# Graph attention and hypergraph convolution on pairs of graphs: row scales through DRAM, score rows and squares transposed, attention moved inside a product chain

## The chip, the cores and the metric

The kernel runs on one core of one Trainium2 chip. The metric is the device time of one execution, in microseconds (us), on the slowest (here the only) core. A single-core program has no second die to compare with, so runs are compared by their spread.

## The reference, cut to what matters

128 graphs of 128 nodes with 512 features. A layer of graph attention (8 heads of 64), then a layer of hypergraph convolution (hidden size 1024), each with a residual and a layer norm. Shortened:

```
feats   = x W                                   # per head: 64 features
e       = leaky_relu(e_self[i] + e_neigh[j])    # scores, 8 heads of 128x128
att     = softmax(e - 1e10*(1 - adj))
y       = layernorm(x + relu(att feats + b))
# hypergraph convolution; w = first row of adj, H = (adj != 0)
Dn      = 1 / sum_e H[n,e] w[e]                 # one scale per node (row)
Be      = 1 / sum_n H[n,e]                      # one scale per edge
S       = diag(Dn) H diag(Be) H^T               # 128x128, used twice
h       = layernorm(relu(S (y W1) + b1))
out     = layernorm(y + S (h W2) + b2 + y)
```

## The kernel before: the parts that the change and the argument touch

The kernel works on pairs of graphs. Every step of a pair is entered with a lag (in periods) and a time in the period, and the program is laid out in the order of these numbers, 39.2 us to a period; so four or five pairs are in work at once, and each engine executes its own instructions strictly in that order. The large products (pf, ph, py) are Strassen-like chains of seven products; ScalarE copies three partial results per chain out of PSUM.

```
# S: rows scaled in SBUF by VectorE, transposed by PE, R = S^T copied out by ScalarE
hD[:, g] = (a[:, g] != 0) * dn[:, g]            # nodes, VectorE, 2 per pair
pa[g]    = PE transpose(hD[:, g])               # 2 per pair
hDT      = ScalarE copy(pa)
pd[g]    = matmul(hB[:, g], hDT[:, g])          # hB = edge-scaled H^T
R        = ScalarE copy(pd)
# score rows: PE transposes e_neigh (16 rows of 128), VectorE copies them out of PSUM,
# two writes to DRAM, then each row is read back by all 128 partitions
rows = copy(pr[:16])
for g in range(2):
    dma rd[g] <- rows[8g:8g+8]                  # 8 partitions x 4 runs of 128 B
for g in range(2):
    dma nb[:, g] <- rd[g] broadcast             # 4 KB runs
# then: GpSimd adds the mask to nb, ScalarE applies leaky relu, VectorE takes the largest
# squares: pm[:, g] = matmul(sq[:, g, 0], mean1)        # one column, 1/DH
# py chain: seven products py(1..7); ScalarE copies out py after the 1st, 3rd and 5th that PE does
# next pair's blocks: four loads xb (x) and four loads ab (adjacency)
```

The steps from load to score rows are all DMAs that one engine, SP, issues in program order.

## Time and profile before

| | before |
|---|---|
| time, median of 3 runs | 2601.62 us (2600.46 to 2602.16) |
| busy: PE, VectorE, ScalarE, GpSimd | 97, 78, 60, 66% |
| steady period (one pair) | 39.12 us, PE busy in all of it |
| chain that ended last | PE 96% |

These are the SP lines of one period of the kernel before (start, length, line, output and input, number of DMAs; the length is that of issuing, with waits inside a group included):

```profile
1087.64 2.47 SPq L110 DMA_DIRECT2D xb<-in_x_dram  x4
1090.16 2.13 SPq L115 DMA_DIRECT2D ab<-in_adj_dram  x4
1093.92 0.62 SPq L470 DMA_DIRECT2D rd<-rows  x2
1095.16 0.82 SPq L479 DMA_DIRECT2D nb<-rd  x2
```

The reader is to see that the score rows are issued 1.6 us after the four ab loads are done, and that the first read of them back follows 1.24 us after the first write began. In the median of 60 periods it is 1.24 us as well, and the four ab loads take 1.94 us.

### The profile page before, as it was taken

Reading aid. Unit: us, or ns where it says so; the run is one execution under the profiler, and the core shown is the slowest. Engines: PE = TensorE matmul, PEld = TensorE weight load, DVE = VectorE, ACT = ScalarE, POOL = GpSimd, SP = SyncE. Lnnn points to the kernel's source line nnn. Section 1 sums busy time; section 2 is a strip of 40 time slices with the busy share of each in tenths; the row PEclk is TensorE's granted clock in tenths of the full one; section 3 lists DMA queues with packets and bytes.
Section 4 is the critical chain, followed back from the end, with each engine's and each line's share of the span. In section 5 each row is a group of like instructions: output and inputs, shape, how many; then the busy total and the mean of one; then the engine's idle time right before and its main releaser. Section 6 shows DMA issues by size and latency. Waiting matters only on the chain.

```text
span 2601.9 us, 48690 instructions
## 1 busy us (share of the span) xinstructions
PE 2530.2 (97%) x16624; PEld 2298.1 (88%) x16624; DVE 2027.5 (78%) x4584; ACT 1555.9 (60%) x4425; POOL 1720.3 (66%) x1809
## 2 busy tenths in 40 slices
PE   4799999999999999999999999999999999999997
PEld 2699999999999999999899999999999999999986
DVE  5788788787788787787787788787787787787773
ACT  2566566566566566566566566566565575575562
POOL 3566766766766766766767767667767667767653
PEclk9899999999999999999999999999999999999998
DMA  6344444443444444443443444444544534534430
GB/s 162 110 130 132 135 130 132 135 130 123 144 130 127 140 129 126 142 130 121 147 129 121 148 127 122 148 126 122 150 124 123 151 122 125 151 120 127 147 106 17
DMA packets 332668, 335.64 MB, mean 129 GB/s; under 512 B 99442, under 2 KB 265346, under 8 KB 332420
## 3 DMA queue, kind: packets, MB, share of 16 engines
q1 hardware_dynamic: 328724, 331.46, 42.3%
q8 instruction: 132, 2.16, 0.3%
q10 hardware_dynamic: 3696, 1.06, 0.2%
q14 instruction: 116, 0.95, 0.1%
HBM read 232.27 MB, written 100.14 MB: 128 GB/s over the span
## 4 chain that ended last, share of the span: by engine, by line
PE 96%; DVE 1%; DMA 1%; issue 1%; POOL 0%; ACT 0%; SPq 0%; POOLq 0%; DVEq 0%; ACTq 0%
PE pyX L419 17%; PE phX L698 17%; PE pfX L419 9%; PE phW L698 9%; PE pyW L419 8%; PE pav L572 8%; PE pz L663 4%; PE phY L698 4%; PE pfW L419 4%; PE pyY L419 4%; PE pq L819 4%; PE pfY L419 2%; PE pd L379 1%; PE pm L792 1%; PE pa L329 1%
## 5 line engine op out<-in xcount | busy, mean ns | idle before, releaser
L290 ACT COPY py<-pyX 128x257 f32<-128x257 f32 (+1 forms) x192 | 71.7, 374 | 561.1 <-PE pyX L419 557.7
L698 PEld LDWEIGHTS phX<-zS,w_sb 128*128 128x128 f32 x3072 | 363.1, 192 | 31.2 <-issue 31.2
L698 PE MATMUL phX<-zS,w_sb 128*128 128x128 f32 x3072 | 374.2, 275 | 0.7 <-issue 0.7
L492 POOL TENSOR_TENSOR nb<-nb,neg 128x512 f32<-128x512 f32 x256 | 320.1, 1271 | 75.7 <-DMA nb<-rd 75.7
L499 ACT ACTIVATE nb<-nb,ft 128x128 f32<-128x128 f32 x1024 | 326.4, 392 | 53.1 <-POOL nb L492 53.0
L749 POOL TENSOR_TENSOR sq<-sq 128x512 f32<-128x512 f32 (+2 forms) x384 | 321.6, 837 | 36.3 <-ACT sq L738 21.1
L513 ACT ACTIVATE nb<-nb,nm 128x128 f32<-128x128 f32 x1024 | 320.4, 395 | 0.0
L619 POOL TENSOR_TENSOR rso<-veo,mhalf 128x2 f32<-128x2 f32 x64 | 44.8, 700 | 375.9 <-DVE veo L617 375.9
L572 PEld LDWEIGHTS pav<-ft,eT 128*128 128x128 f32 x2048 | 253.3, 193 | 11.8 <-DVE eT L534 3.4
L419 PE MATMUL pyX<-w_sb,h 128*128 128x257 f32 (+1 forms) x1024 | 253.6, 390 | 0.2
L572 PE MATMUL pav<-ft,eT 128*128 128x65 f32 x2048 | 247.6, 271 | 3.4 <-DVE eT L534 3.2
L419 PE MATMUL pyX<-w_sb,hS 128*128 128x257 f32 (+1 forms) x1024 | 244.6, 381 | 3.2 <-POOL hS L401 3.2
L419 PE MATMUL pyW<-w_sb,hS 128*128 128x256 f32 x1024 | 242.3, 378 | 0.0
L728 ACT ACTIVATE h<-h,b_sb 128x128 f32<-128x128 f32 x768 | 239.4, 392 | 1.4 <-DVE h L713 1.4
L686 POOL TENSOR_TENSOR zS<-zT 128x256 f32<-128x256 f32 x128 | 93.5, 730 | 210.3 <-ACT zT L675 210.3
L419 PEld LDWEIGHTS pyX<-w_sb,hS 128*128 128x128 f32 x1024 | 194.6, 190 | 32.2 <-POOL hS L401 3.6
L419 PEld LDWEIGHTS pyW<-w_sb,hS 128*128 128x128 f32 x1024 | 193.9, 189 | 28.0
L596 POOL TENSOR_TENSOR y<-y,b_bc 128x512 f32<-128x512 f32 x128 | 186.3, 1456 | 28.5 <-DVE rden L586 24.6
L419 PEld LDWEIGHTS pyX<-w_sb,h 128*128 128x128 f32 x1024 | 185.7, 191 | 21.7 <-ACT py L290 0.4
L505 DVE TENSOR_REDUCE nm<-nb 128x4 f32<-128x512 f32 x256 | 174.2, 681 | 23.3 <-ACT nb L499 22.9
L290 ACT COPY ph<-phX 128x512 f32<-128x512 f32 x192 | 112.4, 585 | 88.9 <-PE phX L698 88.9
L534 DVE STREAM_TRANSPOSE eT<-eb 128x512 f32<-128x512 f32 x252 | 163.0, 683 | 0.1
(125 smaller groups left out, 5846.8 us busy)
## 6 DMA issues: line engine op xcount, KB each, us to landing
nb<-rd SPq DMA_DIRECT2D x128, 512.0 KB
ed<-nb SPq DMA_DIRECT2D x126, 512.0 KB
eb<-ed SPq DMA_DIRECT2D x504, 128.0 KB
xb<-in_x_dram SPq DMA_DIRECT2D x256, 128.0 KB
x<-in_x_dram SPq DMA_DIRECT2D x64, 512.0 KB
out_dram<-o SPq DMA_DIRECT2D x64, 512.0 KB
a<-in_adj_dram SPq DMA_DIRECT2D x64, 128.0 KB
w<-in_adj_dram SPq DMA_DIRECT2D x128, 64.0 KB
```

The source lines that it names most:

```text
L290: nc.scalar.copy(t[:, :n], s[kind, "X"][:, :n])
L419: nc.tensor.matmul(to[:, :n], lhs[:, k, :], rhs[:, k, :n], start=bool(start) and k == 0, stop=(k == nk - 1), skip_group_check=True,)
L492: nc.gpsimd.tensor_tensor(t, t, neg[:, :, None, :].to_broadcast([P, NB, HH, B]), op=ALU.add)
L499: nc.scalar.activation(t, t, AF.Prelu, bias=s["ft"][:, g, h, 0:1], alpha=SLOPE)
L505: nc.vector.tensor_reduce(s["nm"][:, g, hs], scores(p, s, g, hs).rearrange("p b h j -> p h b j"), AX.XY, ALU.max, negate=True,)
L513: nc.scalar.activation(t, t, AF.Exp, bias=s["nm"][:, g, h:h + 1])
L534: nc.vector.transpose(s["eT"][:, g, hs, :].rearrange("p h (b i) -> p h b i", b=NB), s["eb", g][:, :, hs, :].rearrange("p b h j -> p h b j"),)
L572: nc.tensor.matmul(t[:, h * (U + 1):(h + 1) * (U + 1)], s["eT"][:, g, q * HH + h, :], s["ft"][:, g, q * HH + h, 2:], start=True, stop=True,)
L596: nc.gpsimd.tensor_tensor(s["y"][:, g, :], s["y"][:, g, :], b0_bc, op=ALU.add)
L698: nc.tensor.matmul(to[:, m * N:(m + 1) * N], w[:, k, m * P:(m + 1) * P], rhs[:, k, :], start=bool(start) and m == 0 and k == 0, stop=(k == ...
L728: nc.scalar.activation(dst[:, k, :], src[:, k, :], AF.Relu, bias=b1_sb[:, c:c + 1])
L749: nc.gpsimd.tensor_tensor(t[:, :n, :], t[:, :n, :], t[:, n:2 * n, :], op=ALU.add)
```

## The change

Its intent is to take small work off PE, which is the bound. Four parts: (1) S comes from H^T alone, and the row scale Dn is multiplied in along the columns when R leaves PSUM; for that the 256 scales of a pair go through DRAM and are read back by all partitions. (2) Score rows are turned by VectorE's 32x32 block transpose instead of PE. (3) The squares are transposed by PE and summed by VectorE. (4) The two late attention blocks (pav) and the py chain are interleaved otherwise. The diff, cut to its core:

```diff
-        s["hD"] = ...                       # and its two VectorE scalings     (1)
+        s["dn"] = dn
+    @step(0, 16.0)
+    def write_nodes(p, s):
+        s["dd"] = dram.tile([2, N], F32, ...)
+        nc.sync.dma_start(s["dd"].rearrange("g n -> n g"), s["dn"])
+    @step(1, 20.0)
+    def spread_nodes(p, s):
+        s["dnb"] = work.tile([P, 2 * N], F32, ...)
+        nc.sync.dma_start(s["dnb"], s["dd"].rearrange("g n -> (g n)").partition_broadcast(P))
-    def transpose_nodes ...                 # pa, 2 PE transposes
-    def d_evict ...                         # ScalarE copy
-                s["hB"][:, g, :], s["hDT"][:, g, :],
+                s["hB"][:, g, :], s["hT"][:, g, :],
-        nc.scalar.copy(R, pd)
+        nc.vector.tensor_tensor(R, pd, s["dnb"], op=ALU.mult)
 ...
-        pr = PE transpose; rows = copy(pr)  # two writes of 8 partitions       (2)
+        rows = work.tile([P, B], F32, ...)
+        nc.vector.transpose(rows, e_self and e_neigh columns of ft)
+        for b in range(NB):                 # four writes of 16 partitions
+            nc.sync.dma_start(s["rd"][b], rows[b * B + 2 * H:(b + 1) * B])
 ...
-            nc.tensor.matmul(s["pm"][:, g:g + 1], s["sq"][:, g, 0, :], mean1)  # (3)
+            nc.tensor.transpose(s["pm"][:, g * N:(g + 1) * N], s["sq"][:, g, 0, :], ident)
+        nc.vector.tensor_reduce(ve, s["pm"], AX.X, ALU.add)
 ...
-    (..., ((1, 0), 24.2), ((1, 1), 25.0)):  attend                           # (4)
+    (..., ((1, 0), 25.95), ((1, 1), 26.8)): attend
-    chain("py", 3, (26.0, 27.8, 29.5, 31.2, 33.0, 35.5, 37.2, 27.9, 31.4, 34.75), ...
+    chain("py", 3, (24.2, 29.4, 27.7, 32.9, 31.2, 35.35, 37.1, 26.2, 29.6, 33.1), ...
-    T = 39.2
+    T = 38.6
```

More of the change, by code (lines that the diff above doesn't have):

```diff
@@ L176 @@
     nc.gpsimd.memset(mhalf, -0.5)
-    mean1 = const.tile([P, 1], F32, name="mean1")
-    nc.gpsimd.memset(mean1, 1.0 / DH)
     fts = []
@@ L313, in nodes @@
         nc.vector.scalar_tensor_tensor(dn, dd, 0.0, dn, op0=ALU.is_gt, op1=ALU.mult)
-        s["hD"] = work.tile([P, 2, N], F32, tag="hD", name=f"hD_{p}")
-        for g in range(2):
-            nc.vector.tensor_scalar(
-                s["hD"][:, g, :], a[:, g, :], 0.0, dn[:, g:g + 1], op0=ALU.not_equal, op1=ALU.mult
-            )
+        s["dn"] = dn
+    @step(0, 16.0)
+    def write_nodes(p, s):
+        s["dd"] = dram.tile([2, N], F32, tag="dd", name=f"dd_d_{p}")
+        nc.sync.dma_start(s["dd"].rearrange("g n -> n g"), s["dn"])
+    @step(1, 20.0)
+    def spread_nodes(p, s):
+        s["dnb"] = work.tile([P, 2 * N], F32, tag="dnb", name=f"dnb_{p}")
+        nc.sync.dma_start(
+            s["dnb"], s["dd"].rearrange("g n -> (g n)").partition_broadcast(P)
+        )
     @step(0, 38.4)
@@ L323, in mask @@
         nc.gpsimd.tensor_scalar(s["neg"], s["a"], -1.0, BIG, op0=ALU.add, op1=ALU.mult)
-    @step(1, 1.78)
-    def transpose_nodes(p, s):
-        s["pa"] = bank(f"pa_{p}")
-        for g in range(2):
-            nc.tensor.transpose(s["pa"][:, g * N:(g + 1) * N], s["hD"][:, g, :], ident)
     @step(1, 31.0)
@@ L345 @@
     at(1, 5.3, x_transpose, 1)
-    @step(1, 2.6)
-    def d_evict(p, s):
-        s["hDT"] = work.tile([P, 2, N], F32, tag="hDT", name=f"hDT_{p}")
-        nc.scalar.copy(s["hDT"].rearrange("p g n -> p (g n)"), s["pa"][:, :2 * N])
     @step(1, 3.4)
@@ L373, in scale_edges @@
             )
-    @step(1, 34.6)
+    @step(1, 34.7)
     def propagator(p, s):
@@ L379, in propagator @@
             nc.tensor.matmul(
-                s["pd"][:, g * N:(g + 1) * N], s["hB"][:, g, :], s["hDT"][:, g, :],
+                s["pd"][:, g * N:(g + 1) * N], s["hB"][:, g, :], s["hT"][:, g, :],
                 start=True, stop=True,
             )
-    @step(1, 35.3)
+    @step(1, 35.8)
     def r_evict(p, s):
         s["R"] = work.tile([P, 2, N], F32, tag="R", name=f"R_{p}", bufs=3)
-        nc.scalar.copy(s["R"].rearrange("p g n -> p (g n)"), s["pd"][:, :2 * N])
+        nc.vector.tensor_tensor(
+            s["R"].rearrange("p g n -> p (g n)"), s["pd"][:, :2 * N], s["dnb"], op=ALU.mult
+        )
     def first_sums(s, key, name, a, i, engine, tag):
@@ L447, with blocked, spread_rows @@
     at(1, 23.4, f_sum, 1, 0, None, "X")
-    @step(1, 24.95)
-    def transpose_scores(p, s):
-        s["pr"] = bank(f"pr_{p}")
-        nc.tensor.transpose(
-            s["pr"][:2 * H, :N], s["ft"][:, :, :, 1].rearrange("p g h -> p (g h)"), ident
-        )
-    def blocked(p, t):
-        dims = "(h b j) -> {}b h j" if p == 0 else "(b h j) -> {}b h j"
-        if len(t.shape) == 2:
-            dims = "p " + dims.format("p ")
-        return t.rearrange(dims.format(""), b=NB, h=H)
-    @step(1, 25.4)
-    def spread_rows(p, s):
-        rows = work.tile([2 * H, N], F32, tag="rows", name=f"rows_{p}")
-        nc.vector.tensor_copy(rows, s["pr"][:2 * H, :N])
-        rd = s["rd"] = dram.tile([2, NB, H, B], F32, tag="rd", name=f"rd_{p}")
-        for g in range(2):
+    def blocked(p, t):
+        dims = "p (h b j) -> p b h j" if p == 0 else "p (b h j) -> p b h j"
+        return t.rearrange(dims, b=NB, h=H)
+    @step(1, 25.0)
+    def spread_rows(p, s):
+        rows = work.tile([P, B], F32, tag="rows", name=f"rows_{p}")
+        nc.vector.transpose(
+            rows.rearrange("p (c x) -> p c x", c=2),
+            s["ft"][:, :, :, :2].rearrange("p g h c -> p c (g h)"),
+        )
+        shape = [2 * H, NB, B] if p == 0 else [NB, 2 * H, B]
+        s["rd"] = dram.tile(shape, F32, tag="rd", name=f"rd_{p}")
+        for b in range(NB):
             nc.sync.dma_start(
-                blocked(p, rd[g].rearrange("b h j -> (b h j)")).rearrange("b h j -> h b j"),
-                rows[g * H:(g + 1) * H].rearrange("h (b j) -> h b j", b=NB),
+                s["rd"][:, b, :] if p == 0 else s["rd"][b],
+                rows[b * B + 2 * H:(b + 1) * B],
             )
@@ L478, in neighbours @@
         for g in range(2):
-            nc.sync.dma_start(
-                s["nb"][:, g, :],
-                s["rd"][g].rearrange("b h j -> (b h j)").partition_broadcast(P),
-            )
+            hs = slice(g * H, (g + 1) * H)
+            dst, src = s["nb"][:, g, :], s["rd"]
+            if p == 0:
+                src = src[hs].rearrange("h b j -> (h b j)")
+            else:
+                dst = dst.rearrange("p (b x) -> p b x", b=NB)
+                src = src[:, hs, :].rearrange("b h j -> b (h j)")
+            nc.sync.dma_start(dst, src.partition_broadcast(P))
     def scores(p, s, g, hs):
@@ L553 @@
     for (g, q), tm, (lag, tl), (lagx, tx), te, tt in (
-        ((0, 0), 31.0, (1, 32.5), (1, 34.8), 2.7, 18.1), ((0, 1), 33.0, (1, 35.4), (1, 37.3), 4.6, 18.15),
-        ((1, 0), 34.2, (1, 38.0), (2, 2.0), 7.8, 21.5), ((1, 1), 35.4, (2, 6.0), (2, 7.3), 7.9, 21.55),
+        ((0, 0), 31.0, (1, 32.4), (1, 33.9), 2.7, 18.1), ((0, 1), 32.2, (1, 34.0), (1, 36.7), 4.6, 18.15),
+        ((1, 0), 34.2, (1, 37.5), (2, 2.0), 7.8, 21.5), ((1, 1), 35.4, (2, 6.0), (2, 7.3), 7.9, 21.55),
     ):
@@ L575, in attend @@
             )
-    for (g, q), t in (((0, 0), 20.65), ((0, 1), 20.7), ((1, 0), 24.2), ((1, 1), 25.0)):
+    for (g, q), t in (((0, 0), 20.65), ((0, 1), 20.7), ((1, 0), 25.95), ((1, 1), 26.8)):
         at(2, t, attend, g, q)
@@ L592 @@
     at(2, 22.5, attended, 0)
-    at(2, 26.4, attended, 1)
+    at(2, 27.9, attended, 1)
     def add_bias(p, s, g):
@@ L598 @@
     at(2, 24.1, add_bias, 0)
-    at(2, 28.0, add_bias, 1)
+    at(2, 29.2, add_bias, 1)
     def residual(p, s, g):
@@ L625, in normalize @@
         )
-    at(2, 27.6, residual, 0)
-    at(2, 30.0, residual, 1)
-    at(2, 31.7, rstds, "a")
-    @step(2, 32.6)
+    at(2, 26.2, residual, 0)
+    at(2, 30.7, residual, 1)
+    at(2, 32.7, rstds, "a")
+    @step(2, 34.95)
     def first_shift(p, s):
@@ L642, in first_output @@
         )
-    at(2, 37.0, first_output, 0)
-    at(2, 37.1, first_output, 1)
+    at(2, 35.7, first_output, 0)
+    at(2, 35.75, first_output, 1)
     def skip(p, s, g):
@@ L752 @@
         for level in range(3):
-            at(3, ((17.0, 17.1, 17.2), (26.0, 28.5, 28.6))[g][level], squares, g, level)
+            at(3, ((17.0, 17.1, 17.2), (26.0, 27.3, 28.0))[g][level], squares, g, level)
     def h_sums(p, s, i):
@@ L767, in weigh @@
         rows_product(s, i, halves(s["h"], KH // 2), s["hS"], w2_sb, QU, KH // 2, 1, to, start)
-    chain("py", 3, (26.0, 27.8, 29.5, 31.2, 33.0, 35.5, 37.2, 27.9, 31.4, 34.75), weigh,
+    chain("py", 3, (24.2, 29.4, 27.7, 32.9, 31.2, 35.35, 37.1, 26.2, 29.6, 33.1), weigh,
           QU, 1)
@@ L781, in y_sum @@
             nc.vector.tensor_tensor(dst, s["py", i][:, :n], s["py", where][:, :n], op=ALU.add)
-    at(3, 29.6, y_sum, 0, 0, 0, "Y")
-    at(3, 35.4, y_sum, 1, 1, 2, "W")
+    at(3, 31.3, y_sum, 0, 0, 0, "Y")
+    at(3, 34.9, y_sum, 1, 1, 2, "W")
     at(4, 0.1, y_sum, 0, 1, 1, "W")
-    at(3, 37.3, y_sum, 1, 0, None, "X")
-    @step(3, 35.0)
+    at(3, 37.2, y_sum, 1, 0, None, "X")
+    @step(3, 34.8)
     def sum_squares(p, s):
@@ L791, in sum_squares @@
         for g in range(2):
-            nc.tensor.matmul(
-                s["pm"][:, g:g + 1], s["sq"][:, g, 0, :], mean1, start=True, stop=True
-            )
+            nc.tensor.transpose(s["pm"][:, g * N:(g + 1) * N], s["sq"][:, g, 0, :], ident)
     @step(3, 36.0)
@@ L801, in h_rstd @@
         ve = small.tile([P, 2], F32, tag="ve", name=f"veh_{p}")
-        nc.vector.tensor_tensor(ve, s["pm"][:, :2], m2, op=ALU.subtract)
+        nc.vector.tensor_reduce(
+            ve, s["pm"][:, :2 * N].rearrange("p (g f) -> p g f", g=2), AX.X, ALU.add
+        )
+        nc.vector.scalar_tensor_tensor(
+            ve, ve, 1.0 / DH, m2, op0=ALU.mult, op1=ALU.subtract
+        )
         nc.vector.tensor_scalar(ve, ve, 0.0, EPS, op0=ALU.max, op1=ALU.add)
@@ L860, in shift @@
             if lag == 0:
-                return 2.5 if time < 20.0 else 0.0
+                return 2.5 if time < 12.0 else 0.0
             if lag == 1 and 4.0 < time < 10.0:
@@ L866, in shift @@
         if p == 1 and lag == 1:
-            if time < 3.0:
-                return -3.0
+            if time < 4.0:
+                return -6.0
             return -17.5 if time < 10.0 else -13.0 if time < 12.0 else -23.1 if time < 26.0 else 0.0
```

## The prediction

> **What bounds the kernel now.** One core, so no dies to compare; the granted clock is 0.992. I read the busy shares first, then PE's waits over the whole run, then the busy times of one steady period, then the chain of waits inside it.
>
> ```profile
> PE 2530.2 (97%) x16624; PEld 2298.1 (88%) x16624; DVE 2027.5 (78%) x4584; ACT 1555.9 (60%) x4425; POOL 1720.3 (66%) x1809
> ...
> 1025.69:1064.81 39.12, 39.12 (x260) 35.70 (x261) 31.02 (x72) 24.20 (x71) 26.84 (x29) 1.00 0.42 132
> ```
>
> The second line is one period (one pair of graphs; there are 64): PE is busy 39.12 of 39.12 us, VectorE 31.02, ScalarE 24.20, GpSimd 26.84, the DMA engines 42%. PE's waits are all start and end effects, each counted once or twice:
>
> ```profile
> PE pa L329 <- DVE hD L316: 29.9, 1, 29.9
> PE pz L663 <- ACT y L640: 17.5, 1, 17.5
> PE pyX L419 <- POOL hS L401: 3.2, 1, 3.2
> PE pav L572 <- DVE eT L534: 3.2, 1, 3.2
> ```
>
> So from about 92 us to 2523 us the time is the sum of PE's slots, and nothing else counts unless it makes PE wait. The chain of waits gives those slots (start, length); these are the ones the change touches, with their neighbours:
>
> ```profile
> 1029.26 1.78 PE pz L663 x16
> 1031.04 0.22 PE pa L329 x2
> 1031.26 1.79 PE phX L698 x16
> ...
> 1049.94 1.73 PE pav L572 x16
> ...
> 1053.50 0.84 PE pav L572 x8
> 1054.34 0.11 PE pr L452
> 1054.45 0.84 PE pav L572 x8
> 1055.29 1.79 PE pyX L419 x8
> ...
> 1062.29 1.73 PE pyX L419 x8
> 1064.03 0.44 PE pd L379 x4
> 1064.47 0.34 PE pm L792 x4
> 1064.81 1.84 PE pyX L419 x8
> ```
>
> Three things to see. A matmul is two instructions (pd: 2 products, x4), a transpose one (pa: 2, x2), and both cost 0.11 us an instruction at 128 columns (0.44/4, 0.22/2). A product of 128x256 takes 1.73 for 8, or 0.217 each. And a product is longer by what a short predecessor could not hide: pyX is 1.73 after a long one, 1.79 after pav (65 columns), 1.84 after pm (1 column).
>
> **What the Trainium skill says.** "TensorE: Matmul & The Clock Gate", section "LDWEIGHTS (loading the stationary operand)", gives a load as its columns over 1.2, that is 107 ns for 128 columns, and its step-by-step section lets the next load run under the current matmul. The trace agrees: pav streams only 65 columns and yet takes 1.73/16 = 0.108 us, a load's time, and pm with its single column has 0.34 + (1.84 - 1.73) = 0.45 for four loads. The same page, "Part 4: PE-mode transpose", warns that the clock gate does not open for transposes alone; here pa's slots are as short as pd's, so between matmuls that does not show. "VectorE: DVE Perf Modes", section "Why PSUM operands drop a tier", leaves fp32 from PSUM at one element a cycle; VectorE's sums from PSUM took 0.42 us at 256 columns and 0.685 at 512, a slope of 0.97 elements/ns, which fits, and I use these rows for the new PSUM reads. "SBUF — State Buffer", section "SBUF: two separate sides", says that VectorE with two SBUF inputs and a GpSimd operation lock each other out of a port pair. The trace has the like: first_shift on 128x2 elements lasts 1.20 us on average beside GpSimd's score additions, but 0.16 at 2548.94 when GpSimd is idle.
>
> **The change part by part.** All in us per period.
> 1. S from H^T alone. Two PE transposes (pa) go: -0.22. The propagator still has 2 products of 128x128, 0.44. The row scale is now multiplied in as PSUM is left, so ScalarE loses two copies (0.38 + 0.37), VectorE loses the hD scaling (two, 0.48 together) and gets a 128x256 product from PSUM (0.42). The scales go through DRAM: one write of 256 single floats and one broadcast read of 128 KB. They are written about a period before use, so I charge them nothing.
> 2. Score rows by VectorE's transpose. PE's pr goes: -0.11. But pr with its 128 columns also hid one load between two pav blocks: 0.84 + 0.11 + 0.84 = 1.79, whereas 16 in one block cost 1.73. Net -0.06. VectorE loses a copy (0.28) and gets a 128x32 transpose: from 0.434 at 256 elements and 0.683 at 512, about 0.434 - 224 x 0.00097 = 0.22.
> 3. Squares. pm with its after-effect, 0.45, becomes two transposes of 128 columns, 0.22, after which the next load is hidden: -0.23. VectorE pays a 128x256 reduction from PSUM, about 0.43 (from 0.68 at 512), and a tiny operation takes the place of a tiny one.
> 4. Attention inside the py chain. The four pav blocks and the py products stay the same, and each of the two pav stretches is still followed by one uncovered load. The move gives cover: the ScalarE copy between py's first and third product now hides behind pav (1.73), as it did behind the second product. PE's sum does not move: 0.
>
> PE: -0.22 - 0.06 - 0.23 = -0.51, so 39.12 becomes 38.61. VectorE: +0.42 - 0.48 - 0.28 + 0.22 + 0.43 = +0.31, to 31.3 of 38.6, 81%. ScalarE: 23.4. Neither is a bound.
>
> One term is paid back. Without pa, phX follows pz directly and must have zT, which ScalarE copies out of pz. The trace shows that very sequence in the last periods, where there is no pa any more:
>
> ```profile
> 2515.94 1.78 PE pz L663 x16
> 2517.72 1.83 PE phX L698 x16
> ```
>
> phX is 1.83 instead of 1.79. I take 0.04 back: -0.47, a period of 38.65. Over some 62 dense periods that is -29 us.
>
> The ends. At the start the chain from 56 to 77 us is VectorE, dense with weight preparation; the change puts the edge work of pair 1 (about 1.3) and the new eviction there (0.42), takes out hD (0.48), and orders residual 0 ahead of attended 1, so that each waits once more for GpSimd's 1.26 us addition. I take +2 before the first dense period. At the end, py's third product (the one that needs GpSimd's hS) now comes ahead of the second, so the second (1.74) no longer fills the wait for hS of the last pair: +1.7, less 0.4 for each of two ScalarE copies that are covered now: +1. Sum: 2601.6 - 29 + 3 = 2575.6; I say 2575, a ratio of 1.010.
>
> **The rivals.**
> A. The wait for zT takes more than 0.04. ScalarE's order at the end of a period is leaky, first_output, the y copy, leaky, zT. In the steady state before, the zT copy waited 0.41 for PE:
>
> ```profile
> 1030.18 0.58 ACT L675 COPY zT<-pz 128x512 f32<-128x512 f32 x1 [0.41 <-PE pz L663]
> ```
>
> That is all the slack there was, beside the 0.22 of pa. With a period 0.5 shorter the same ScalarE chain, fed by VectorE's first_shift, may reach zT after pz. Against: the eviction of R has left ScalarE and first_output is scheduled 1.3 earlier. If it costs 0.3 a period the time is 2575 + 62 x 0.26 = 2591; if it ate all of the gain, about 2604.
> B. The scores arrive late. nb was already waited for:
>
> ```profile
> 1060.16 1.27 POOL L492 TENSOR_TENSOR nb<-nb,neg 128x512 f32<-128x512 f32 x1 [1.25 <-DMA nb<-rd]
> ```
>
> The row write becomes four issues for two (0.31 each), which eats the 0.5 that the shorter VectorE path gives, and the broadcast reads 1 KB pieces where it had 4 KB. From here the chain is GpSimd mask, ScalarE leaky, ScalarE's third py copy, PE's sixth py product. In my layout of the new period the copy is free at 33.5 after pz's start and its result is needed at 35.2, so some 1.3 are spare after the copy itself. A delay of 1 costs nothing, one of 2 some 0.7 a period, giving about 2618.
> C. VectorE at 81% becomes the bound through port locks. For: it has many long small operations. Against: of the new ones, two read PSUM and the third is small, and its slack is 7 a period. I give it little; 2590 at most.
> D. All goes better: no payback at phX, the ends neutral. Then 2601.6 - 0.51 x 63 = 2569.5. To pass 2% (2549.6) a period would have to lose 0.84 and PE holds only 0.67 + 0.11 of the removed work, before what is added: nearly impossible unless the reordering removes overheads that the slots do not show.
>
> **Range and chances.** D sets the near end, 2564 with a few us for starts I misjudged; A in its milder form the far end, 2592. Faster by over 2%: 0.03. Within 2%: 0.94. Slower by over 2% (2653, a new wait of 1.3 us each period): 0.03.
>
> **What would show it.** The steady period should be 38.6 to 38.7 with PE still busy throughout. In the chain, pa and pr are gone, pm is x2 at 0.22, the pyX after it is 1.73, the two late pav blocks read x16 at 1.73 between two pyX, of which the second is 1.79, and phX after pz 1.83. VectorE should show about 31.3 and ScalarE 23.4 a period. Wrong would be: a pm slot far above 0.22 (then step 3 falls); phX well above 1.83 with a wait on zT (A); pyX with a wait on the py copy while GpSimd waits longer for nb (B); first PE work of the dense stretch several us later than 92 us, or a last wait for hS far from 5 us (then the ends are misjudged).

## The result, and the profile after

The changed kernel took 3002.46 us (median of 6 runs, 2983.67 to 3008.82), the kernel before 2601.88 in the same rounds (6 runs). Ratios here and below are the mean time of one kernel's runs over that of the other's of the same rounds, so not quite the ratio of the medians that are quoted: 1.1529, with a 95% interval of 1.1498 to 1.156. It is 15% slower; 2575 was predicted (the prediction's ratio of 1.010 is before over after, the other way round).

The page of the changed kernel, busy shares and the shares of the chain that ended last (in the kernel before PE had 96% of that chain):

```profile
PE 2639.9 (88%) x16304; PEld 2356.4 (78%) x16304; DVE 2037.0 (68%) x4584; ACT 1522.1 (51%) x4297; POOL 1722.8 (57%) x1808
...
PE 45%; DMA 26%; POOL 7%; issue 6%; DVE 6%; SPq 6%; ACT 4%; DVEq 0%; POOLq 0%; ACTq 0%
```

PE has 320 instructions less, as intended, and yet is busy 110 us longer; and the chain now runs through DMAs for a quarter of the span. Ten periods of before and a stretch of the same length after; columns are the window, its length, then busy us and instructions of PE, its weight loads, VectorE, ScalarE and GpSimd, the granted clock, the DMA share and GB/s:

```profile
1000.00:1391.20 391.20, 391.20 (x2592) 357.02 (x2591) 312.01 (x712) 242.11 (x691) 268.33 (x280) 1.00 0.43 132
```
```profile
1000.00:1391.00 391.00, 347.91 (x2176) 311.97 (x2175) 270.06 (x611) 205.72 (x583) 227.92 (x239) 0.95 0.50 117
```

PE now idles 11% of the time, and the granted clock has dropped to 0.95. Every engine has done 14 to 16% fewer instructions in the same time: no engine has become the bound, all wait. The period, from one pz to the next, has gone from 39.12 to about 45.4 us on average (42 to 48), where 38.65 was predicted. The waits of the changed kernel, one line for each link (engine, line and output, what it waited for: us in total, times, longest us):

```profile
PE pyX L417 <- ACT py L288: 280.1, 62, 7.6
```
```profile
ACT nb L497 <- POOL nb L490: 557.9, 63, 26.5
POOL nb L490 <- DMA nb<-rd: 230.8, 40, 10.0
```
```profile
SPq L115 <- DMA dd_d<-dn: 139.3, 51, 5.5
SPq L115 <- DMA out_dram<-o: 92.0, 56, 3.3
SPq L480 <- DMA rd<-rows: 85.6, 82, 3.2
```

Read from the top: PE waits 4.5 us a period (280.1/62) for a ScalarE copy of py; ScalarE stands before its leaky relu and waits for GpSimd's masked scores; GpSimd waits for nb, the scores read back; and SP, which issues all this, waits 139 us in front of the **ab loads** for the write of the row scales to land, and 92 us for the output write that was issued behind it. Of the three SP waits only the last was there before, with 35.5 us in all. The chain of waits in one period shows the same as times:

```profile
1081.07 10.41 DMA xb<-in_x_dram
1091.50 0.30 SPq L464
1091.84 3.51 DMA rd<-rows
1095.43 4.37 DMA nb<-rd
1099.87 1.27 POOL nb L490
...
1101.47 0.97 ACT nb L497 x3
1102.44 0.27 ACT py L288
1102.75 3.73 PE pyX L417 x8
1106.48 1.73 PE pyW L417 x8
```

Note two things. The copy py takes 0.27 us in this chain, but stands behind four leaky relus in ScalarE's in-order queue. And the py product after the wait takes 3.73 us for 8 instructions instead of 1.73: after standing still PE is slow at first, so a wait of 4.5 us costs some 2 us more. SP's own lines of that period, to be held against those of before:

```profile
1076.35 0.38 SPq L317 DMA_DIRECT2D dd_d<-dn  x1
...
1079.11 2.40 SPq L110 DMA_DIRECT2D xb<-in_x_dram  x4
1081.56 7.96 SPq L115 DMA_DIRECT2D ab<-in_adj_dram  x4
1089.57 0.45 SPq L322 DMA_DIRECT2D dnb<-dd_d  x1
1090.31 1.96 SPq L464 DMA_DIRECT2D rd<-rows  x4
1095.43 0.93 SPq L480 DMA_DIRECT2D nb<-rd  x2
```

The four ab loads take 7.96 us instead of 2.13, and rows-written to rows-read takes 5.12 us instead of 1.24. Those are the two places where the time comes from. In the median they are 6.0 against 1.94, and 3.6 against 1.24. The first is the larger, and its cause is a write of 1 KB:

```profile
dd_d<-dn SPq DMA_DIRECT2D x64, 1.0 KB, 9.8
```

The last column is the median time from issue to landing: 9.8 us for 256 single floats. The view knows the landing of only 33 of the 64 writes. The packed trace also holds every update of the semaphores; taking the last update before a semaphore's next DMA gives all 64: 9.7 us in the median, 8.0 to 13.9. Where a landing below is said to be read from the semaphores, it is read in this way.

### The profile page after: what moved, and what is told of

The parts are those of the page before. It is cut to its first block, busy times and chain, and to the rows that moved or that the text cites. A ratio compares the mean times of both kernels' runs of the same rounds, so it can differ in the third digit from the quotient of the medians. Undisturbed runs are those within 1.5% of the kernel's fastest.

```text
span 3007.0 us, 48421 instructions
## 1 busy us (share of the span) xinstructions
PE 2639.9 (88%) x16304; PEld 2356.4 (78%) x16304; DVE 2037.0 (68%) x4584; ACT 1522.1 (51%) x4297; POOL 1722.8 (57%) x1808
## 3 DMA queue, kind: packets, MB, share of 16 engines
q8 instruction: 130, 2.13, 0.4%
## 4 chain that ended last, share of the span: by engine, by line
PE 45%; DMA 26%; POOL 7%; issue 6%; DVE 6%; SPq 6%; ACT 4%; DVEq 0%; POOLq 0%; ACTq 0%
PE phX L696 15%; DMA xb<-in_x_dram 11%; PE pyX L417 8%; PE phW L696 6%; DMA nb<-rd 6%; PE pyW L417 5%; PE pz L661 4%; PE phY L696 4%; DMA rd<-rows 4%; PE pq L820 3%; SPq L110 3%; DVE o L620 3%; DMA ab<-in_adj_dram 3%; POOL nb L490 3%; POOL hS L399 2%
## 5 line engine op out<-in xcount | busy, mean ns | idle before, releaser
L417 PE MATMUL pyX<-w_sb,h 128*128 128x257 f32 (+1 forms) x1024 | 339.1, 489 | 280.1 <-ACT py L288 280.1
L417 PEld LDWEIGHTS pyX<-w_sb,h 128*128 128x128 f32 x1024 | 244.1, 245 | 339.6 <-ACT py L288 294.9
L747 POOL TENSOR_TENSOR sq<-sq 128x512 f32<-128x512 f32 (+2 forms) x384 | 343.0, 893 | 44.6 <-ACT sq L736 24.5
L417 PE MATMUL pyW<-w_sb,hS 128*128 128x256 f32 x1024 | 269.6, 410 | 0.0
L417 PEld LDWEIGHTS pyW<-w_sb,hS 128*128 128x128 f32 x1024 | 220.7, 216 | 40.9
L601 DVE SCALAR_TENSOR_TENSOR y<-y,x 128x512 f32<-128x512 f32 x128 | 154.5, 1207 | 126.2 <-POOL y L594 125.8
L594 POOL TENSOR_TENSOR y<-y,b_bc 128x512 f32<-128x512 f32 x128 | 162.5, 1270 | 123.9 <-DVE y L585 100.7
```

The costliest lines, as they stand in the source:

```text
L417: nc.tensor.matmul(to[:, :n], lhs[:, k, :], rhs[:, k, :n], start=bool(start) and k == 0, stop=(k == nk - 1), skip_group_check=True,)
L594: nc.gpsimd.tensor_tensor(s["y"][:, g, :], s["y"][:, g, :], b0_bc, op=ALU.add)
L601: nc.vector.scalar_tensor_tensor(y, y, 0.0, s["x"][:, g, :], op0=ALU.max, op1=ALU.add)
L747: nc.gpsimd.tensor_tensor(t[:, :n, :], t[:, :n, :], t[:, n:2 * n, :], op=ALU.add)
```

## The experiments

The theory after reading the trace: the row-scale write lands late, and holds SP in front of the ab loads; a smaller part comes from part 2's score rows. Rivals: the changed order (part 4) starves PE, or the larger DMA traffic does. All kernels gave right results, except one that says so. Each time below stands beside runs of the kernel before on the same chip.

### Which part costs the time

**e1_no_part1**: the changed kernel with part 1 undone.

```diff
-  write_nodes, spread_nodes, VectorE product with dnb
+  hD, transpose_nodes (pa), d_evict, ScalarE copy of R
```

> The changed kernel with its first part undone: hD, its two PE transposes and the two ScalarE copies are back, the write and the broadcast read of the row scales are gone; score rows, squares and the py order stay changed. Theory 1 (the write of 256 single floats, which took 9.8 us to land, holds the SP queue, so that the score rows are written some 5 us late and PE waits for the third py copy behind the late scores): about 2585 us, no wait of pyX for the py copy, issue of the four ab loads back to some 2 us. Theory 2 (the four row writes and the 1 KB broadcast pieces make the scores late): still about 2950 to 3000. Theory 3 (the new py order leaves no slack for the copy behind leaky, whatever the DMA): still above 2800.

2618.22 us (2616.7 to 2621.83), ratio 1.0067. The shortest period is 38.84 us: the predicted savings of parts 2 and 3 (0.06 + 0.23) from 39.12 make 38.83. So 384 us of the loss are in part 1, and the rival of part 4's order, which is still in, falls with them; but 16 us over before remain, with PE waiting 20.6 us for py's copy.

**e2_write_only**: the kernel before, with nothing added but the write of the scales, which nobody reads.

```diff
+    @step(0, 16.0)
+    def write_nodes(p, s):
+        s["dd"] = dram.tile([2, N], F32, ...)
+        nc.sync.dma_start(s["dd"].rearrange("g n -> n g"), s["dn"])
```

> The kernel before with nothing but the write of the row scales (256 single floats to DRAM at the same place in the SP queue) added; nobody reads it. Theory 1: the ab loads are issued some 5 us later, nb lands 3 to 5 us later, PE waits 2 to 4 us a period for the py copy and then runs cold: 2750 to 2950 us. Theories 2 and 3: within 0.5% of the kernel before, 2602 us.

2852.67 us, ratio 1.0957 (1.093 to 1.0983). One DMA of 1 KB a pair, read by nobody and computing nothing, costs 251 us. PE waits 134.3 us for py's copy in 52 periods, and SP's ab loads are held as in the changed kernel (138.6 us for the scale write, 97.1 for the output write):

```profile
1070.44 6.20 SPq L115 DMA_DIRECT2D ab<-in_adj_dram  x4
```

**e3_write_late**: the changed kernel, with the write later in the period.

```diff
-    @step(0, 16.0)
+    @step(0, 32.0)
     def write_nodes(p, s):
```

> The changed kernel with the write of the row scales moved in the SP queue from ahead of the x blocks (time 16) to behind the residual's loads (time 32), when the queue is otherwise idle and the scores have already been read; everything else as changed. Theory 1: about 2576 us, PE dense again with a period near 38.65. Theories 2 and 3: no better than 2950. A rival within theory 1, that the write slows whatever lies beside it on the DMA engines: in between, since the loads of a and w then come late.

2635.04 us, ratio 1.0127. One number in the program order takes back 367 us of the loss. The ab loads are back at 1.94 us in the median.

**e4_rows_write**: the scales transposed by VectorE first, and written as four DMAs of two runs of 128 bytes.

```diff
-        nc.sync.dma_start(s["dd"].rearrange("g n -> n g"), s["dn"])
+        for b in range(NB):
+            nc.sync.dma_start(s["dd"][:, b * B:(b + 1) * B], s["dn"][b * B:b * B + 2])
```
(with dn in a 128x32 tile, transposed by VectorE into s["dn"])

> The changed kernel with the row scales transposed by VectorE (32x32 blocks of a 128x32 tile) and written as 8 runs of 128 bytes in four issues at the same place of the SP queue, in place of 256 single floats in one issue. Theory 1: about 2576 us (plus 0.24 us of VectorE a period, which costs nothing). If it is the place in the queue or the mere extra issues that hold it, not the 256 single floats: still far above 2700. Theories 2 and 3: about 3000.

2633.19 us, ratio 1.0125. The same as moving the write. So part 1 can be had with its write harmless, and what remains over before, 32 us, is not in the write. The larger DMA traffic is in this kernel too (344 MB, before 336), so it is not what cost the 369 us.

### What the slow write does to SP

**e12_write_on_act_queue**: the changed kernel, with the write issued by ScalarE.

```diff
-        nc.sync.dma_start(s["dd"]..., s["dn"])
+        nc.scalar.dma_start(s["dd"]..., s["dn"])
```

> The changed kernel with only the slow write (256 single floats) issued by ScalarE instead of SP, at the same time. If the 9.8 us of that write hold only SP's own queue: SP's ab loads go out in 2 us again, time near e4_rows_write, 2630. If the write holds the DMA engines that all queues share: the loads behind it still land late, and the time stays above 2800.

2953.38 us, ratio 1.1348: only 49 us better. SP still waits for the write, although the write is not on its queue any more:

```profile
SPq L110 <- DMA dd_d<-dn: 235.9, 61, 9.6
```

So it is not the queue that holds SP. The second forecast, that the loads behind the write still land late, came true beside it: more on this below. Line 110 is xb, where the wait was at ab (line 115) before; why that is so comes next.

**What the program says.** All DMAs of this program, whichever engine issues them, take turns on eight completion semaphores, and before a DMA may use one, its issuer waits until the DMA that used it last has landed. So **every DMA waits for the one eight before it**. In the changed kernel, for pair 20 (semaphore, count waited for, in the order of the program):

```
dd_d(20) <- dn       waits for semaphore 5 >= 1216, signals 5 (+16)
out <- o(16)                           6 >= 1216,          6
xb(20) <- x   x4                       7, 0, 1, 2
ab(20) <- adj #1                       3 >= 1232,          3
ab(20) <- adj #2                       4 >= 1232,          4
ab(20) <- adj #3                       5 >= 1232,          5    <- 1216 + 16: dd_d has landed
ab(20) <- adj #4                       6 >= 1232,          6    <- out has landed
```

The third ab load needs the row-scale write, the fourth the output write: these are the two waits of line 115 in the table above. In e12 the write takes semaphore 1 some places earlier, and the third **xb** load is eight behind it: line 110. In e3 the DMA eight behind is the fourth eb load of the attention matrix, which comes after the landing of a later write anyway, and nothing is held. The third ab load comes some 6 us after the write: in the SP lines above, 1081.56 plus two issues of 0.53 (2.13/4), less 1076.35, makes 6.3. A write that lands within 6 to 7 us costs nothing; one of 9.8 holds SP some 3 (2.7 on average where it waited, 139.3/51). The ab loads became longer by 4.1 (6.0 - 1.94). Over the 64 periods that is 2.2 for the scales (139.3/64), 1.4 for the output write (92.0/64), and the rest in waits that the view puts down to eb loads (29.7/64). The chain of waits above goes from an xb load to the row writes for the same reason: the first three row writes have xb loads eight before them. The number of semaphores was not varied in any run; that the ring explains where the wait stands in three placements (ab, xb, none) is what supports it.

**A second effect of the same write.** What is issued behind it lands late as well, and that is why the fourth ab load has to wait for an output write at all. The output write and the x loads in the changed kernel, then in f2 (below), where the scales land early:

```profile
xb<-in_x_dram SPq DMA_DIRECT2D x256, 128.0 KB, 8.7
out_dram<-o SPq DMA_DIRECT2D x64, 512.0 KB, 8.6
```
```profile
xb<-in_x_dram SPq DMA_DIRECT2D x256, 128.0 KB, 3.6
out_dram<-o SPq DMA_DIRECT2D x64, 512.0 KB, 3.2
```

In e12 the output write still takes 7.3 us, although the slow write was issued by another engine; so the delay is in something that both queues share. In e3 it is the loads of a and w, now behind the write, that land late (11.1 and 10.4 us, before 6.1 and 5.7, read from the semaphores), and there it costs next to nothing: VectorE waits 2.9 us for w in the whole run. In the changed kernel both effects are at work, the ring by 139.3 us of SP's waits and the late landing by 92.0 us; no run separates what each is worth in kernel time.

### Why the write lands so late

Four writes of e2's kind, with another layout. The place in the program is e2's, and so is the order of the semaphores.

**f2_write_spread**: each of the 256 floats into 512 bytes of DRAM of its own.

```diff
-        s["dd"] = dram.tile([2, N], F32, ...)
-        nc.sync.dma_start(s["dd"].rearrange("g n -> n g"), s["dn"])
+        s["dd"] = dram.tile([N, 2, P], F32, ...)
+        nc.sync.dma_start(s["dd"][:, :, 0], s["dn"])
```

> The write alone added to the kernel before, as in e2_write_only (2853 us), still 256 single floats, but each into its own 512 bytes of DRAM instead of all into two runs of 512 bytes. If the single floats are slow because they collide in the same lines of DRAM: near 2602. If it is the number of pieces, or their being small, whatever the address: 2853 again.

2604.82 us, ratio 1.0013 (0.9996 to 1.003), against 2852.67 of e2. As many pieces, as small, from the same tile: only the addresses differ. Read from the semaphores, the 64 writes land in 2.65 us in the median, against 9.6 in e2, and the ab loads take 1.93 us. (The view gives 5.1 us here, but knows only two of the 64 landings, of the first two pairs, 7.4 and 2.8; so it is for f3 and f4 too.) In one period:

```profile
1091.75 2.27 SPq L115 DMA_DIRECT2D ab<-in_adj_dram  x4
```

So neither the number of pieces nor their size alone makes the write late: it needs that they are packed into the same kilobyte of DRAM.

**f3_write_pairs**: both floats of a node side by side, 128 pieces of 8 bytes in 1 KB.

```diff
-        s["dd"] = dram.tile([2, N], ...);  dma s["dd"].rearrange("g n -> n g") <- s["dn"]
+        s["dd"] = dram.tile([N, 2], ...);  dma s["dd"] <- s["dn"]
```

> The write alone added to the kernel before, with the two scales of a node side by side in DRAM: 128 pieces of 8 bytes instead of 256 of 4, the same 1 KB in all. If the time of the write goes by the number of pieces: half the hold, about 2650 to 2730. If it goes by collisions in the same lines: little gain, above 2750.

2609.39 us, ratio 1.0028. Read from the semaphores it lands in 3.9 us (median); the ab loads take 2.28 us. Half as many pieces in the same kilobyte, and the write is in time. Both forecasts missed. Over f2's 2.65 us the write needs 1.2 us more, where e2 needs 7.0: far less than half. So to share the kilobyte is not enough either; what size of stretch or of piece counts, no run tells.

**f4_write_128x128B**: 128 pieces of 128 bytes, 16 KB (of hD; nobody reads it).

```diff
+        s["dd"] = dram.tile([N, B], ...);  dma s["dd"] <- s["hD"][:, 0, :B]
```

> The write alone added to the kernel before, now 128 pieces of 128 bytes (16 KB; other data, never read). By the number of pieces: as f3_write_pairs. If bytes or a piece's size cost: different from f3; were it the smallness of 4 or 8 bytes that is slow, this one is near 2602 and f3 is not. By collisions in lines (4 pieces to 512 bytes here instead of 64): near 2605.

2609.18 us, ratio 1.0025; landing median 2.65 us (from the semaphores), ab loads 1.93. Sixteen times the bytes of e2 land in under a third of its time.

**f1_pairs_in_changed**: f3's write in the changed kernel (read back in one run and used through a strided view).

```diff
-        s["dd"] = dram.tile([2, N], F32, ...)
+        s["dd"] = dram.tile([N, 2], F32, ...)
```

> The changed kernel with one repair: the two scales of a node lie side by side in DRAM (128 pieces of 8 bytes), the broadcast reads them as they lie, and the product on leaving PSUM picks them with a stride. If the write of 256 single floats into two runs of 512 bytes is all that separates the changed kernel (3002) from e4_rows_write (2633): 2625 to 2660, the four ab loads issued in 2 to 2.5 us.

2638.88 us, ratio 1.0139, 363 us better than the changed kernel; the write lands in 3.7 us (median). A layout of one kilobyte is worth 363 us here.

### The rest: the score rows

**e8_part2_only**: the kernel before with part 2 alone.

```diff
-  pr = PE transpose; copy; two writes of 8 partitions x 4 runs; reads of 4 KB runs
+  VectorE transpose; four writes of 16 partitions x 1 run; reads of 1 KB runs
```

> The kernel before with the second part alone: score rows by VectorE's transpose, four writes, 1 KB pieces. By PE's slots 0.06 a period less: 2598. If the four writes land late in a part of the periods, as in e1 and e4, nb comes up to 2.5 us later there against a slack of 1.4: some 10 to 20 periods with a wait of about 1 us for the py copy, 2605 to 2630.

2613.65 us, ratio 1.004 (1.0025 to 1.0055). The period is 39.06 to 39.07 us nearly everywhere, the 0.06 of the prediction to the digit; and yet it is 11 us slower, of which 9.2 are ten waits for py's copy. From the first row write to the first read there pass 2.85 us (median), where it was 1.24.

**e6_no_part2**: e4 with part 2 undone.

```diff
-  VectorE transpose; four writes of 16 partitions; reads of 1 KB runs
+  pr = PE transpose (between pyX and pav); copy; two writes; reads of 4 KB runs
```

> As e4_rows_write, with the second part undone: the score rows come from PE's transpose again and are written by two DMAs of 32 runs each and read in 4 KB runs, in place of four writes of 16 runs and 1 KB pieces. If the four writes' landing (2.8 us after the last issue in the bad periods, against at most 1.1 in the kernel before) is the second cause: PE's waits for the py copy vanish and the time is about 2585 (0.06 a period more for pr). If the new py order has too little slack in itself: still about 2630.

2597.45 us, ratio 0.9982 (0.9967 to 0.9997). Part 2 costs 36 us in e4. The period is 38.78 us nearly throughout. The chain of waits of this kernel shows parts 1, 3 and 4 working as predicted; pa is gone, pm is x2 at 0.22, the pyX after it 1.73 and phX after pz 1.83:

```profile
1028.15 0.22 PE pm L798 x2
1028.37 1.73 PE pyX L425 x8
...
1031.84 1.78 PE pz L669 x16
1033.62 1.83 PE phX L704 x16
```

**f6_rows_scattered**: e4 with each 128-byte piece of a write in 512 bytes of its own, and 4 KB read runs for all pairs. Its result is wrong (relative error 0.94): the heads are read in an order that the later steps don't expect.

```diff
-        shape = [2 * H, NB, B] if p == 0 else [NB, 2 * H, B]
+        shape = [2 * H, NB, B]
```

> As e4_rows_write (2633 us), but each of the 16 pieces of 128 bytes of a score-row write goes to its own 512 bytes of DRAM (heads outermost) instead of all into one run of 2 KB; the read is then one run of 4 KB per partition and the scores are permuted, so the result is wrong on purpose. If pieces that fall close together in DRAM are what is slow, as for the row scales: first row write to issue of nb falls from 3.2 us to some 1.6 to 2.0, and the time to 2580 to 2595. If it is the place of the transposed rows in SBUF (16 partitions of one block): 3.2 us and 2625 to 2640 as before.

2617.44 us, ratio 1.0053. First write to first read stays at 3.23 us (e4: 3.21). So the addresses, which decided about the scales, have nothing to do with this delay. 16 us are gained; the reads in runs of 4 KB are all else that differs, but that was not tried alone.

**f5_rows_four_writes**: four writes with part 2 left out (e10 below), each of 4 partitions of 4 runs.

```diff
-            nc.sync.dma_start(<rd[g]>, <rows[g*8:(g+1)*8]>)            # two writes
+            for q in range(2):
+                nc.sync.dma_start(<rd[g], heads q>, <rows, 4 of the 8>)  # four writes
```

> As e10_orders_no_part2 (2590 us; PE's transpose, score rows written by two DMAs of 32 runs of 128 bytes), with the same rows written by four DMAs of 16 runs each. If it is the number of small writes that makes the scores late in e9_orders (2659): the first row write to the issue of nb goes from 1.2 us to about 3 to 5 and the time rises to 2620 to 2660. If it is where the transposed rows lie (partitions 16 to 31 of each block of 32): 2590 to 2595.

2589.05 us (2587.56 to 2594.26), ratio 0.9951. Four writes, and first write to first read is 1.57 us. So it is not their number either. SP's lines of one period of e8, then of f5:

```profile
1096.19 1.71 SPq L466 DMA_DIRECT2D rd<-rows  x4
1099.01 0.93 SPq L482 DMA_DIRECT2D nb<-rd  x2
```
```profile
1090.45 1.28 SPq L477 DMA_DIRECT2D rd<-rows  x4
1091.97 1.58 SPq L487 DMA_DIRECT2D nb<-rd  x2
```

The program resolves it: it is **which writes the first read waits for**. Before, the read of graph 0 waits for the write of graph 0 alone, the first one; the second is still in flight. In f5 it waits for two of four. With part 2 every write holds a block of nodes of both graphs, so the first read waits for all four. A write lands about a microsecond after its issue: before, 1.24 - 0.31 = 0.93 after the first issue's end; in f5, 1.57 - 2 x 0.32 = 0.93 after the second's; in e8, 2.85 - 1.71 = 1.14 after the fourth's. What is left is the issue: 1.71 us for four against 0.31 for one. Part of that is in the issue itself, 0.42 us for a write of 16 partitions where one of 8 takes 0.29 and one of 4 also 0.29; why, no run tells. The account rests on the program's waits and on these sums; no run changed only which writes the first read waits for.

### Can other orders win the time back

**e5_copy_first**: e4 with the first leaky relu behind the third py copy on ScalarE.

```diff
-        ((0, 0), 31.0, (1, 32.4), ...
+        ((0, 0), 31.0, (1, 33.2), ...
```

> As e4_rows_write (row scales written as 128-byte runs), and ScalarE does the third py copy ahead of the first leaky instead of behind it (leaky of heads 0 to 3 from 32.4 to 33.2 in the order). What e4 has left of PE's waits is 33 us for the py copy in 36 periods. If these come from ScalarE taking its queue in order, with the leaky of late scores in front of the copy: they vanish, and the time falls to 2580 to 2592 (start some 6 us later than before, the rest by the slots). If the late scores simply delay everything behind them, first_output and the y of the next pz too: the wait moves to pz and the time stays near 2630.

2630.24 us, ratio 1.0107: the same as e4 within their spreads. The wait for py's copy is gone, and others have come: 16.5 us before phX for zT, 12.8 before pyW for y. Its best periods, without such a wait, are 38.66 to 38.67 us, with all four parts in. That is the predicted period, 38.65.

**e7_copy_first_slow_write**: the same reordering in the changed kernel with its slow write.

```diff
-        ((0, 0), 31.0, (1, 32.4), ...
+        ((0, 0), 31.0, (1, 33.2), ...
```

> The changed kernel as it is, slow write included, with only the third py copy moved ahead of the leaky on ScalarE. The scores are 5 to 7 us late here. The in-order account says that pyX then no longer waits for the copy, but that the lateness reaches PE one stage on, at pz through first_output, which is also behind leaky: PE waits for y in most periods, by 2 to 5 us, and the time lies between 2750 and 2950. If instead the time falls near 2600, the order on ScalarE was the whole cause and the write only its trigger.

2936.24 us, ratio 1.1277. Of 401 us over before, 66 are won. The lateness is still there, and meets PE at another place:

```profile
PE pyW L417 <- DVE y L779: 226.2, 62, 6.2
```

**e9_orders**: e5 with a second leaky relu and a maximum moved back too, so that no copy stands behind a late score.

```diff
-        ((0, 0), 31.0, (1, 33.2), (1, 33.9), ...    ((1, 0), 34.2, (1, 37.5), ...
+        ((0, 0), 31.0, (1, 33.2), (1, 36.6), ...    ((1, 0), 34.2, (2, 1.15), ...
-        (65.0, prepare_output, ())
+        (64.2, prepare_output, ())
```

> As e5_copy_first, and the two further places where a late score stands in an engine's queue ahead of work that PE needs are changed: VectorE takes the first maximum (largest of heads 0 to 3) behind y_sum and first_shift instead of ahead of them (33.9 to 36.6), ScalarE takes the third leaky behind the first zT copy instead of ahead of it (37.5 to 1.15 of the next period), and the start's small pv product is prepared before the second x transpose. If queue order is what turns late scores into PE waits: pyW's wait for y (12.8 us in 21 periods) and phX's wait for zT (16.5 us in 44) are gone, the period is 38.66 nearly throughout, and the time 2575 to 2585, below the kernel before. If lateness only moves on once more: 2610 or above, with another wait named.

Missed: 2659.04 us, ratio 1.0219, slower than e5. The wait has moved on again, to pz before the next pair (22.3 us for ScalarE's y, in 33 periods); the median period is 39.94 us. The later scores are always in front of something.

**e10_orders_no_part2**: the same orders in e6, where the scores come in time.

```diff
   (e6, with the three moves of e9)
```

> As e6_no_part2 (score rows by PE's transpose, two writes) with the same three changes of order as e9_orders. Its steady period is 38.78 by e6. In-order account: the 10 waits of e6 go, 2580 to 2588. Slower than e9_orders by 0.12 x 62 = 7 us if e9_orders reaches its period throughout, faster than it if the four writes still cost something there.

2590.08 us, ratio 0.9953 (0.994 to 0.9965). With scores in time the same orders gain 7 us on e6, where with late scores they lost 29 on e5. This one beats both kernels; f5, its variant with four writes, has the same time (2589.05).

**e11_rows_two_queues**: e9 with two of the four row writes issued by ScalarE.

```diff
-            nc.sync.dma_start(
+            (nc.sync, nc.scalar)[b % 2].dma_start(
```

> As e9_orders with two of the four score-row writes issued by ScalarE instead of SP, so that the four issues take about 0.9 us instead of 1.7. If the four issues' own time makes the scores late, nb comes 0.8 us earlier and SP's wait for the last row write shrinks; the time is as e9_orders or up to 5 us below. If the landing itself is what varies (1.3 to 3 us), no difference.

Missed by far: 2751.08 us, ratio 1.058. The aim was to shorten the issue. SP got a new wait, in front of the ab loads once more:

```profile
SPq L115 <- DMA rd<-rows: 133.5, 60, 3.6
```

In the program ScalarE's first row write takes semaphore 7 between SP's xb loads, and the fourth ab load is eight behind it: SP now waits, before it may load blocks, for score rows that VectorE hasn't made yet. The ring of eight again.

| kernel | us, median | ratio |
|---|---|---|
| changed | 3002.46 | 1.1529 |
| e2: before + the scale write | 2852.67 | 1.0957 |
| f2: the same, 512 B for each float | 2604.82 | 1.0013 |
| e4: changed, scales written as 128 B runs | 2633.19 | 1.0125 |
| e6: e4 without part 2 | 2597.45 | 0.9982 |
| e10, f5: e6 with other orders | 2590.08, 2589.05 | 0.9953, 0.9951 |

## Why the prediction was wrong, point by point

**The bound and PE's sum: right.** The slots came out as given, in the changed kernel too (pm x2, phX 1.83). Periods: part 2 alone 39.06 (predicted 39.06), parts 2 to 4 38.84 (38.83), all four 38.66 where nothing is late (38.65). Part 4 changed nothing in PE's slots; no run has it alone. VectorE's new operations cost what was priced, too: 0.41, 0.24 and 0.41 us in e3 (priced 0.42, 0.22 and 0.43).

**The step that failed:** "The scales go through DRAM: one write of 256 single floats and one broadcast read of 128 KB. They are written about a period before use, so I charge them nothing." It looked at who reads the result. The write does come in time for its reader. What it delayed was an unrelated load, the third ab load, which is eight DMAs behind it in the ring of semaphores; and a write of that layout took 9.8 us to land, more than the 6 to 7 us that the program leaves it; the output write behind it landed late as well and held the fourth ab load. That hold made score rows, scores, masks, ScalarE's leaky relu and the py copy behind it late, and PE waited 4.5 us a period and ran slow after it. It is worth about 369 of the 427 us between prediction and result (3002 against e4's 2633). Such shares hold for the order in which things are undone: added alone to the kernel before, the write costs 251 us (e2), and part 2 costs 11 (e8).

**Rival B was the right mechanism, and mis-sized.** "A delay of 1 costs nothing, one of 2 some 0.7 a period": the wait came exactly as B says, pyX for the py copy while GpSimd waits for nb. The slack of 1.3 fits e8, where the delay of 1.6 (2.85 - 1.24) makes only occasional waits. But the row writes were charged 0.6 ("four issues for two (0.31 each)"), where the first read had to wait for all four in place of one: 4 x 0.42 - 0.31 = 1.4 more issue, and 0.2 more landing. That is the second term, 36 us (e4 against e6), and it should have been seen in the diff: the reads of graph 0 name all blocks.

**The other rivals.** A (zT) showed itself only where the py copy was moved ahead, 16.5 us in all in e5 and 6.4 in e7. C did not become the bound, but VectorE grew by more than its sum. In the changed kernel, which stands still much of the time, its busy time rose by only 9.5 us, 0.15 a pair against +0.31 predicted; in e3, the four parts without the hold, it rose by 42.4 us, 0.66 a pair (the residual's addition takes 1.22 us there instead of 0.70), and in e10 it is busy for 83%. ScalarE's fell by 0.62 in e3 against 0.75 predicted.

**The ends:** the start was taken too lightly. The first pz starts at 95.1 us in e3 against 88.6 before, 6.5 and not 2. The end came as forecast: the last wait for hS is 5.0 us (3.2 before).

**The sum, done again:** 2575, + 8 because e10 keeps pr (38.78 instead of 38.65, 62 periods), + 2 for its start (92.8 - 88.6 = 4.2, of which 2 were counted), makes 2585; e10 measured 2590. In its profiled execution (2594) twelve periods are longer than 38.78, by 6.5 us together, which is about what is left; why, was not followed up. From there e6's orders add 7, part 2 adds 36 (e4) and the scale write 369: 3002. The range of 2564 to 2592 and 3 in 100 for "slower" had no room for a DMA that holds its issuer: a small transfer was judged by its bytes and its reader alone.

## What to carry to other kernels

Before a DMA is called free because its result is needed late, ask what its issuer will wait for while it is in flight: here each DMA waited for the one eight places before it, so a 1 KB write of single floats that landed in 9.8 us held up loads that had nothing to do with it, and made what was issued behind it land late. Write such small data transposed to runs of 128 bytes, or spread, or place it where the eighth DMA after it is late anyway; and when writes are cut otherwise, check how many of them the first read now waits for. When a wait moves on with each reordering, mend its source, not the order.

## What the Trainium skill lacked or had wrong

- "DMA: Bandwidth & Descriptors", section "Specifications", gives 512 bytes as the smallest transfer for line rate, and says that below it the DMA engines read, modify and write. It does not say that small pieces are far worse where they share such a stretch of DRAM: 256 single floats landed in 9.6 us (median) in two runs of 512 bytes, and in 2.65 us with 512 bytes for each, which was worth 248 us of kernel time (2852.67 against 2604.82). That read-modify-write of shared stretches is the cause is not shown: 128 pieces of 8 bytes in the same kilobyte landed in 3.9 us.
- The same page, section "Issuing engines are not separate DMA queues", says that DMAs share the same 16 engines whoever issues them, and that another issuer saves issue time only. The runs agree: nearly nothing was won by it (e12 still 1.1348), and the output write landed in 7.3 us behind a slow write that another engine had issued. But it lacks that another issuer may bring a new wait: two row writes moved to ScalarE made SP wait 133.5 us for them, and the kernel 92 us slower (e11 against e9). No page has the ring of eight completion semaphores that this program's DMAs share, in which a slow DMA stops the issue of the eighth after it; with the late landing behind it, it lengthened four loads' issue from 1.94 to 6.0 us.
- No page has the time to issue a small write by its shape: 0.42 us with 16 partitions of one 128-byte run, 0.29 with 8 or 4 partitions of four.
